# A message-passing layer on one core: bucket regions of a scratch table laid into one another

## The chip, the core and the metric

The kernel runs on one core of a Trainium2 chip. The metric is the device time of one execution in microseconds (us); of several timed runs the median counts. A profile is one further execution under the hardware profiler.

## The reference

The layer works on 12,500 nodes with 64 features and 212,500 edges, sorted by their destination. `src` and `dst` are the two ends of an edge; the sums are made per `src`.

```python
h = jnp.maximum(_layernorm(x, axis=-1), 0.0)
edge_in = jnp.concatenate([h[src], h[dst], edge_weight1], axis=1)
e = jax.nn.silu(edge_in @ eW1 + eb1)
e = jax.nn.silu(e @ eW2 + eb2)
agg = jax.ops.segment_sum(e, src, num_segments=h.shape[0])
node_in = jnp.concatenate([h, agg], axis=1)
x = x + jax.nn.silu(node_in @ nW1 + nb1) @ nW2 + nb2
```

The first matrix product is split: `h @ eW1` of either end is made once per node (the tables `ta` for `src` and `tb` for `dst`, each as three bf16 parts), so that an edge only needs a row of each and its weight times the last row of `eW1`.

## The kernel before, in words

**Buckets.** Nodes are dealt into NB = 100 buckets of L = 125 (node number modulo 100 is the bucket, the quotient is the place in it). Edges come in the order of `dst`, but the sums go by `src`. So edges are first sent to a scratch table in HBM by the bucket of their `src`, and then read back bucket by bucket.

**Chunks.** The edges are cut into blocks of BLK = 1024 and these into 11 chunks (`CHUNKS`, L49): the first has 8 blocks, the others 20 each (the last a little fewer). Each chunk has its own scratch table `q` (L79) of rows of W = 144 floats (576 bytes): 128 floats of the edge's first product so far, and 16 copies of the place of its `src`. A bucket has a region of `cap` x 128 rows in it (cap is 1 in the first chunk, 2 in the others), all of one bucket after one another.

**Zeros.** A bucket doesn't fill its region, so the rows from number `zero` on (48 of 128, then 152 of 256) are written with zeros first. `fill` (L87) does it with DMAs from a tile of zeros, `each` buckets a DMA; a bucket's tail is cut into 64 pieces, one from each of 64 partitions: 234 floats (936 bytes), in the first chunk 180 (720 bytes). Chunk 0's zeros are SP's first DMA (L208); those of chunk c + 1 go out from ACT's queue (L467, 25 buckets a DMA, four DMAs a chunk) in the first blocks of chunk c.

**Prologue** (to L319). SP loads `x`, ACT's queue the edge lists. Layer norm on VectorE and ScalarE, transposes and the table `tb` on TensorE, stores of `tb` and of the transposed `h` (`hd`) by SP. From the edge lists come, per edge, the bucket number of `src` and the place in it, transposed into `bkE` and `locE` (edges on partitions). L313 turns the bucket number b in `bkE` into the last row number before the bucket's region, b * cap * 128 - 1.

**Sending** (`count`, `send`, `send_all`, L389 to L478). For a block of 1024 edges: `load` (L372) brings the block's numbers on all partitions (`bc`), the window of `tb` rows that its `dst` can have (`win`), and the edge weights. VectorE marks the bucket of each edge (L397) and counts the edges of each bucket by a running sum (scan, L400), with the count carried on over the chunk; L407 keeps each edge's own rank, starting with 1. TensorE brings the rank onto the edge's partition by a product with a column of ones (L426) and makes the edge's row from `pick` and `win` (L434). ScalarE copies it to `qs` (L441) and adds the place (L448); VectorE adds rank and region start to the row number `to` (L444); GpSimd scatters 128 rows by an indirect DMA (L453), eight a block, 1661 in all. `qs` has eight buffers of four such tiles.

**Steps.** The scratch table is read in batches of G = 4 buckets. `fetch` (L488) loads a batch's rows from SP's queue (`qt`, L498: on each partition, for each of the four buckets, `n` = cap rows that lie together) and the batch's rows of `ta` (`a3`, L503), NQ = 5 batches ahead. A batch has n steps of 4 x 128 edges; there are 525 steps. A step brings the place onto the columns (`s_lr`, L520), compares (`s_one_t`, L525), adds the transposed row and the `ta` row (`s_pt`, L534 and L541), applies silu (L545), compares the place with the node numbers (`s_one`, L552), makes the second product on top of the bias (L566, L572), applies silu (L576), and sums by place in PSUM (`s_seg`, L586); at the end of a batch `s_add` (L597) adds the sums to `aggT`. Of the last chunk each batch is followed by the node part (`nodes`, L333 to L353).

**Order.** In this main part the order of instructions on TensorE, VectorE, ScalarE and SP is the program's own: `turn` (L604) gives the pieces of a step with how many steps ahead each runs; at six places in it the sending of the next chunk is moved on by so many pieces that the chunk is sent when its first fetch comes (L649 to L667), and `feed` makes the table `ta`, from reloaded parts of `hd` (`hr`, L611), which the first fetches need. While chunk 0 is sent there are no steps yet.

Of the kernel before, what the change touches and what calls it, by code (L numbers as in the profile page):

```python
# [28 lines left out]
F32 = mybir.dt.float32  # L29
F16 = mybir.dt.float16  # L30
# [3 lines left out]
OP = mybir.AluOpType  # L34
# [4 lines left out]
P = 128  # L39
L = 125  # L40
WL = 112
BLK = 1024
# [15 lines left out]
def tile_gnn(ctx: ExitStack, tc: tile.TileContext, x, src, dst, ew, eW1, eb1, eW2, eb2, nW1, nb1, nW2, nb2, out):  # L58
# [14 lines left out]

    chunks = []
    p0 = 0
    for np_, cap, zero in CHUNKS:
# [2 lines left out]
        p0 += np_  # L81


    zeros = const.tile([P, 4 * W], F32, name="zeros")
    nc.gpsimd.memset(zeros, 0.0)

    def fill(c, engine, each):  # L87


        _, _, cap, zero, q = chunks[c]  # L90
        n = (cap * P - zero) * W // 64
        rows = q[: NB * cap * P, :].rearrange("(b s) w -> b s w", s=cap * P)
        for b in range(0, NB, each):
            part = rows[b : min(b + each, NB), zero:, :].rearrange("b s w -> b (s w)")
            part = part.rearrange("b (r n) -> r b n", n=n)
            yield lambda part=part: engine.dma_start(part, zeros[:64, None, :n].to_broadcast(list(part.shape)))

# [48 lines left out]
    nc.vector.tensor_copy(nodes1, nodes_i)  # L146
    ones = const.tile([1, P], F32, name="ones")
    nc.vector.memset(ones, 1.0)
    ones16 = const.tile([P, 1], F16, name="ones16")
    nc.vector.memset(ones16, 1.0)  # L150
    bad = const.tile([P, 2], F32, name="bad")
    nc.vector.memset(bad, 0.0)

# [47 lines left out]
    with tc.tile_pool(name="pro", bufs=1) as pro, tc.tile_pool(name="norm", bufs=2) as np_, tc.tile_pool(  # L201
# [3 lines left out]
        for c0 in range(0, NB, CH):  # L205
            nc.vector.memset(xs[96:, c0 : c0 + CH, :], 0.0)
            rows16(nc.sync.dma_start, xs[:, c0 : c0 + CH, :], x_rows[:, c0 : c0 + CH, :])
        for f in fill(0, nc.sync, NB):  # L208
            f()


# [98 lines left out]
                    nc.scalar.copy(to[:, k0 : k0 + 4, :], tr)  # L310
        for p0, p1, cap, _, _ in chunks:
            v = bkE[:, :, p0:p1]
            nc.vector.tensor_scalar(v, v, float(cap * P), -1.0, op0=OP.mult, op1=OP.add)  # L313


        d3 = pro.tile([P, 3, H], BF16, name="d3")
# [40 lines left out]
    with tc.tile_pool(name="ld", bufs=4) as ld, tc.tile_pool(name="ld2", bufs=NQ) as ld2, tc.tile_pool(  # L357
# [31 lines left out]
        def count(s):  # L389

            if s >= nblocks:
                return
            c = chunk_of[s]
            bc, win, pick = blk[s]
            nc.vector.tensor_scalar(pick[:WL, :], bc[:WL, 0, :], part[:WL, :], None, op0=OP.is_equal)
            oh = wk.tile([NB, BLK], F16, name="oh")
            nc.vector.tensor_scalar(oh, bc[:NB, 1, :], part[:NB, :], None, op0=OP.is_equal)  # L397
            yield
            run = wk.tile([NB, BLK], F16, name="run")
            nc.vector.tensor_tensor_scan(  # L400
                run, oh, nil.to_broadcast([NB, BLK]), carry.get(c, 0.0), op0=OP.add, op1=OP.add
            )
            yield
            n = min(BLK, E - s * BLK)
            end = run[:, n - 1 : n]
            carry[c] = end
            nc.vector.scalar_tensor_tensor(oh, run, 1.0, oh, op0=OP.mult, op1=OP.mult)  # L407
            blk[s].append(oh)
            if s + 1 == nblocks or chunk_of[s + 1] != c:
                u = wk.tile([NB, 1], F32, name="u")  # L410
                for limit, op in ((chunks[c][2] * P, OP.is_gt), (chunks[c][3], OP.is_lt)):
                    nc.vector.tensor_scalar(u, end, float(limit), None, op0=op)
                    nc.vector.tensor_tensor(bad[:NB, 1:2], bad[:NB, 1:2], u, op=OP.add)
            yield

        def send(s):

            p, g = s // 2, s % 2
            c = chunk_of[s]
            _, _, cap, _, q = chunks[c]  # L420
            _, win, pick, run = blk.pop(s)
            n = min(BLK, E - s * BLK)
            nt = -(-n // P)
            rank = misc[:, (s % 2) * TB : (s % 2 + 1) * TB]
            for t in range(nt):
                nc.tensor.matmul(rank[:, t : t + 1], run[:, t * P : (t + 1) * P], ones16[:NB, :], start=True, stop=True)  # L426
            yield
            for t0 in range(0, nt, G):
                qs = qsp.tile([P, G, W], F32, name="qs")
                qp = mm.tile([P, G, H], F32, name="qp", tag="mm")  # L430
                m = min(G, nt - t0)
                for t in range(m):
                    for i in range(3):
                        nc.tensor.matmul(  # L434
                            qp[:, t, :],
                            pick[: WL + 3, (t0 + t) * P : (t0 + t + 1) * P],
                            win[: WL + 3, i, :],
                            start=i == 0,
                            stop=i == 2,
                        )  # L440
                nc.scalar.copy(qs[:, :m, :H], qp[:, :m, :])  # L441
                if t0 == 0:
                    to = top.tile([P, TB], I32, name="to")
                    nc.vector.scalar_tensor_tensor(  # L444
                        to[:, :nt], rank[:, :nt], float(cap * P + 1), bkE[:, g * TB : g * TB + nt, p], op0=OP.min, op1=OP.add
                    )
                at = g * TB + t0
                nc.scalar.copy(  # L448
                    qs[:, :m, H:], locE[:, at : at + m, p][:, :, None].to_broadcast([P, m, W - H])
                )  # L450
                for t in range(t0, t0 + m):
                    k = min(P, n - t * P)
                    i = nc.gpsimd.indirect_dma_start(  # L453
                        out=q[:],
                        out_offset=bass.IndirectOffsetOnAxis(ap=to[:k, t : t + 1], axis=0),
                        in_=qs[:k, t - t0, :],
                        in_offset=None,
                    )

                    tc.declare_no_dep(i.ins, group=f"rows{c}", reason="each edge has a row of its own")  # L460
                    tc.add_to_no_dep_group(f"rows{c}", i.ins)
                yield

        def send_all(c):

            mine = [s for s in range(nblocks) if chunk_of[s] == c]
            zeros_left = list(fill(c + 1, nc.scalar, 25)) if c + 1 < len(chunks) else []  # L467
            each = -(-len(zeros_left) // len(mine))
            for s in mine:
                load(s + 2, 1)  # L470
# [17 lines left out]
        def fetch(i):  # L488
            if i >= len(batches):
                return  # L490
            c, B, n = batches[i]
            assert pending[c] == 0
            while B not in done_a:
                next(feed)
            q = chunks[c][-1]
            at = B * G * n * P
            qt = ld2.tile([P, G * most, W], F32, name="qt")
            nc.sync.dma_start(  # L498
                qt[:, : G * n, :].rearrange("p (b j) w -> p b (j w)", b=G),
                q[at : at + G * n * P, :].rearrange("(b p j) w -> p b (j w)", b=G, p=P),  # L500
            )
# [12 lines left out]
        def s_lr(k):  # L514
            (qt, _, _), tiles = of(k)
# [31 lines left out]

        def s_one(k):
            (qt, _, _), tiles = of(k)
            j = tiles[0][0]  # L550
            one = wk.tile([P, G, L], F32, name="one")
            nc.vector.tensor_tensor(  # L552
                one,
                nodes1[:, None, :].to_broadcast([P, G, L]),
                qt[:, j : j + G, H : H + 1].to_broadcast([P, G, L]),
                op=OP.is_equal,
            )
            st[k]["one"] = one
            c, B, n, g = steps[k]
            if g == n - 1:  # L560
                fetch(c * (NB // G) + B + NQ)

# [259 lines left out]
```

## Time and profile before

| | us |
|---|---|
| median of 3 timed runs | 2777.59 (2777.4 to 2782.52) |
| profiled execution, its own time | 3318.54 |
| its span, first to last instruction | 3316.8 |
| first scatter (L453) starts | 172.5 |
| first step's silu (L545) starts | 303.0 |
| last scatter starts | 3019.2 |

The profiled execution takes longer than the timed ones. On the page, busy times are per engine with their share of the span; PE is TensorE's products, PEld its weight loads, SP only issues DMAs. q1 is SP's DMA queue, q10 ACT's, q0 GpSimd's, q8 brings instructions; the share of a queue is that of all 16 DMA engines over the span. In a table of windows, each engine has its busy time and the number of its instructions; PEclk is the granted clock, then come the DMA engines' mean busy share and GB/s. In a line of a timeline: start, duration, engine and line, and in brackets how long the engine was idle before, and what ended that. A line of the waits gives the total, the number and the longest.

### The profile page before, as it was taken

The page shows a single profiled execution, that of the slowest core. Times are in us where ns is not written, and L with a number is a line of the kernel's source. Part 1 is how long each engine was busy: PE and PEld are TensorE (multiplying, and loading weights), DVE is VectorE, ACT ScalarE, POOL GpSimd, SP SyncE. Part 2 cuts the span into 40 slices and gives each one's busy share as a digit, 9 for nine tenths or more (in the row PEclk, how much of TensorE's full clock was granted, in tenths as well). Part 3 has the DMA queues.
Part 4 walks back from the last instruction along what each step waited for, and adds up shares of the span by engine and source line. Part 5 has one row for each costly group of instructions (what it writes and reads, how often), then busy time and mean ns, then how long its engine had stood idle before and what let it go on. Part 6 is the DMA issues. An engine that isn't in the chain of part 4 may idle for free. (4 is left out here: it accounts for less than half of the span.)

```text
span 3316.8 us, 60674 instructions
## 1 busy us (share of the span) xinstructions
PE 2676.8 (81%) x23583; PEld 2376.4 (72%) x23583; DVE 1891.0 (57%) x2663; ACT 1252.8 (38%) x2663; POOL 1800.1 (54%) x1691
## 2 busy tenths in 40 slices
PE   2575877887888788788888888888887878889998
PEld 1354666777777777777777777777777777778886
DVE  6643565665666566556565655666565656655332
ACT  3422333333343344333333333343333433434443
POOL 1064766666666666566666666656666666662000
PEclk9998777898898988888888888889888888989999
DMA  6567657656755855755675585576557454554441
GB/s 178 183 197 210 199 173 234 194 171 196 227 180 171 247 168 179 233 183 167 191 226 170 176 243 169 166 222 202 179 182 235 160 185 163 185 174 158 133 134 49
DMA packets 388689, 612.83 MB, mean 185 GB/s; under 512 B 47232, under 2 KB 294401, under 8 KB 387877
## 3 DMA queue, kind: packets, MB, share of 16 engines
q1 hardware_dynamic: 269560, 423.47, 40.2%
q0 software_dynamic: 53760, 122.94, 10.7%
q10 hardware_dynamic: 65074, 62.46, 7.6%
q8 instruction: 188, 3.08, 0.4%
q14 instruction: 107, 0.88, 0.1%
HBM read 393.49 MB, written 215.18 MB: 184 GB/s over the span
## 5 line engine op out<-in xcount | busy, mean ns | idle before, releaser
L453 POOL DMA_INDIRECT q<-qs,to x1661 | 1787.4, 1076 | 1203.9 <-ACT qs L448 527.8
L525 DVE TENSOR_SCALAR oneT<-lr,part 125x512 bf16<-125x512 f32 x525 | 392.5, 748 | 666.6 <-remote 251.3
L545 ACT ACTIVATE e<-pt 128x512 f32<-128x512 f32 x525 | 314.7, 599 | 1185.2 <-PE pt L541 349.1
L586 PE MATMUL seg<-one,e 128*128 128x125 f32 x4200 | 658.7, 300 | 75.7 <-issue 63.5
L572 PE MATMUL p<-w,e 128*128 128x128 f32 x4200 | 658.2, 299 | 63.9 <-issue 61.1
L572 PEld LDWEIGHTS p<-w,e 128*128 128x128 f32 x4200 | 582.8, 211 | 105.8 <-issue 97.7
L586 PEld LDWEIGHTS seg<-one,e 128*128 128x128 f32 x4200 | 583.3, 211 | 92.3 <-issue 84.6
L541 PE MATMUL pt<-oneT,a 125*128 125x256 bf16 (+1 forms) x3300 | 498.3, 287 | 67.8 <-issue 65.1
L434 PE MATMUL qp<-win,pick 115*128 115x128 bf16 x4983 | 433.9, 238 | 136.2 <-issue 112.1
L434 PEld LDWEIGHTS <-pick 115*128 115x128 bf16 x4983 | 363.8, 108 | 177.6 <-issue 170.9
L400 DVE TENSOR_TENSOR_SCAN run<-oh,run,misc 100x1024 f16<-100x1024 f16 x197 | 460.9, 2340 | 30.3 <-remote 15.2
L541 PEld LDWEIGHTS <-a 125*128 125x128 bf16 x3300 | 332.2, 105 | 140.8 <-issue 97.5
L534 PE MATMUL pt<-ident,qt 128*128 128x128 f32 x2100 | 365.3, 296 | 76.0 <-DVE oneT L525 38.0
L441 ACT COPY qs<-qp 128x512 f32<-128x512 f32 x416 | 244.0, 586 | 456.8 <-remote 180.0
L597 DVE TENSOR_TENSOR aggT<-aggT,seg 128x500 f32<-128x500 f32 x250 | 168.4, 673 | 394.8 <-PE seg L586 127.0
L576 ACT ACTIVATE e<-p 128x512 f32<-128x512 f32 x525 | 315.4, 601 | 166.8 <-PE pt L534 53.8
L552 DVE TENSOR_TENSOR one<-nodes,qt 128x500 f32<-128x500 f32 x525 | 351.9, 670 | 0.5 <-PE seg L586 0.5
L566 ACT COPY p<-b2f 128x512 f32<-128x512 f32 x525 | 312.9, 596 | 0.0
L534 PEld LDWEIGHTS pt<-ident,qt 128*128 128x128 f32 x2100 | 246.0, 153 | 93.0 <-issue 49.9
L520 PE MATMUL lr<-identb,qt 128*125 128x128 bf16 x2100 | 234.2, 233 | 42.7 <-issue 36.2
L407 DVE SCALAR_TENSOR_TENSOR oh<-run,oh 100x1024 f16<-100x1024 f16 x208 | 253.6, 1219 | 0.0
L520 PEld LDWEIGHTS <-qt 128*125 128x125 bf16 x2100 | 206.0, 149 | 55.7 <-issue 51.0
(117 smaller groups left out, 1266.4 us busy)
## 6 DMA issues: line engine op xcount, KB each, us to landing
qt<-q SPq DMA_DIRECT2D x250, 576.0 KB
a<-ta SPq DMA_DIRECT2D x275, 384.0 KB
bc<-rows SPq DMA_DIRECT2D x208, 448.0 KB
q<-zeros ACTq DMA_DIRECT2D x40, 1462.5 KB
q<-qs,to POOLq DMA_INDIRECT x1661
win<-tb SPq DMA_DIRECT2D x208, 84.0 KB
tb<-parts SPq DMA_DIRECT2D x25, 384.0 KB
ta<-parts SPq DMA_DIRECT2D x25, 384.0 KB
```

Of the source, the lines that this page charges most:

```text
L400: nc.vector.tensor_tensor_scan(run, oh, nil.to_broadcast([NB, BLK]), carry.get(c, 0.0), op0=OP.add, op1=OP.add)
L434: nc.tensor.matmul(qp[:, t, :], pick[: WL + 3, (t0 + t) * P : (t0 + t + 1) * P], win[: WL + 3, i, :], start=i == 0, stop=i == 2,)
L453: i = nc.gpsimd.indirect_dma_start(out=q[:], out_offset=bass.IndirectOffsetOnAxis(ap=to[:k, t : t + 1], axis=0), in_=qs[:k, t - t0, :], in ...
L520: nc.tensor.matmul(lr[:L, t, :], loc[:, at : at + 1].to_broadcast([P, L]), identb, start=True, stop=True)
L525: nc.vector.tensor_scalar(oneT, st[k].pop("lr")[:L], part1[:L, :], None, op0=OP.is_equal)
L534: nc.tensor.matmul(pt[:, t, :], qt[:, j, :H], ident, is_transpose=True, start=t == 0, stop=False, skip_group_check=True)
L541: nc.tensor.matmul(pt[:, cols, :], a3[:L, b, i, :], oneT[:, cols, :], start=False, stop=i == 2, skip_group_check=True)
L545: nc.scalar.activation(e1, pt, AF.Silu)
L552: nc.vector.tensor_tensor(one, nodes1[:, None, :].to_broadcast([P, G, L]), qt[:, j : j + G, H : H + 1].to_broadcast([P, G, L]), op=OP.is_e ...
L572: nc.tensor.matmul(p2[:, t, :], e1[:, t, :], w2, start=False, stop=t == G - 1, skip_group_check=True)
L576: nc.scalar.activation(e2, p2, AF.Silu)
L586: nc.tensor.matmul(item[2][:, b, :], e2[:, t, :], one[:, t, :], start=j % n == 0, stop=j % n == n - 1)
```

## The change

The regions of the four buckets of a batch are laid into one another: row r of bucket b, which had row number b * cap * 128 + r, now has (b // 4) * 4 * cap * 128 + 4 * r + b % 4. So the four buckets' rows that one partition of `qt` takes lie together in HBM, and so do the zeros of four buckets.

- `fetch`: one run of 4 x n rows per partition, 4608 bytes (2304 in the first chunk) in place of four of 1152 (576). Inside `qt` the rows are now ordered by rank and then bucket, so `of` gives other tile numbers, `s_one` reads the places with one more dimension, and `s_seg` starts and stops its sums at other tile numbers.
- `fill`: pieces of 3744 bytes (2880 in the first chunk), in DMAs of 7 groups of four buckets (7, 7, 7, 4) in place of 25 buckets; as many DMAs and bytes as before. The tile of zeros has 936 floats a partition in place of 576.
- The row number needs b // 4: three further VectorE instructions per chunk in the prologue. The rank is multiplied by 4 (`fours` in place of `ones16`), and starts with 0.

```diff
-    zeros = const.tile([P, 4 * W], F32, name="zeros")
+    most_zeros = max((cap * P - zero) * G * W // 64 for _, cap, zero in CHUNKS)
+    zeros = const.tile([P, most_zeros], F32, name="zeros")
...
-        n = (cap * P - zero) * W // 64
-        rows = q[: NB * cap * P, :].rearrange("(b s) w -> b s w", s=cap * P)
-        for b in range(0, NB, each):
-            part = rows[b : min(b + each, NB), zero:, :].rearrange("b s w -> b (s w)")
+        n = (cap * P - zero) * G * W // 64
+        rows = q[: NB * cap * P, :].rearrange("(b s) w -> b s w", s=cap * P * G)
+        for b in range(0, NB // G, each):
+            part = rows[b : min(b + each, NB // G), zero * G :, :].rearrange("b s w -> b (s w)")
...
-    ones16 = const.tile([P, 1], F16, name="ones16")
-    nc.vector.memset(ones16, 1.0)
+    fours = const.tile([P, 1], F16, name="fours")
+    nc.vector.memset(fours, float(G))
...
-        for f in fill(0, nc.sync, NB):
+        for f in fill(0, nc.sync, NB // G):
...
-            nc.vector.tensor_scalar(v, v, float(cap * P), -1.0, op0=OP.mult, op1=OP.add)
+            q4 = np_.tile([P, 2 * TB, p1 - p0], F32, name="q4")
+            nc.vector.tensor_scalar(q4, v, 0.5 - G / 2, 1.0 / G, op0=OP.add, op1=OP.mult)
+            nc.vector.tensor_scalar(q4, q4, float(3 * 2**22), None, op0=OP.add)
+            nc.vector.tensor_scalar(q4, q4, -float(3 * 2**22), None, op0=OP.add)
+            nc.vector.scalar_tensor_tensor(v, q4, float(cap * P * G - G), v, op0=OP.mult, op1=OP.add)
...
-                run, oh, nil.to_broadcast([NB, BLK]), carry.get(c, 0.0), op0=OP.add, op1=OP.add
+                run, oh, nil.to_broadcast([NB, BLK]), carry.get(c, -1.0), op0=OP.add, op1=OP.add
...
-                        to[:, :nt], rank[:, :nt], float(cap * P + 1), bkE[:, g * TB : g * TB + nt, p], op0=OP.min, op1=OP.add
+                        to[:, :nt], rank[:, :nt], float(G * cap * P), bkE[:, g * TB : g * TB + nt, p], op0=OP.min, op1=OP.add
...
-            zeros_left = list(fill(c + 1, nc.scalar, 25)) if c + 1 < len(chunks) else []
+            zeros_left = list(fill(c + 1, nc.scalar, 7)) if c + 1 < len(chunks) else []
...
-                qt[:, : G * n, :].rearrange("p (b j) w -> p b (j w)", b=G),
-                q[at : at + G * n * P, :].rearrange("(b p j) w -> p b (j w)", b=G, p=P),
+                qt[:, : G * n, :].rearrange("p j w -> p (j w)"),
+                q[at : at + G * n * P, :].rearrange("(p j) w -> p (j w)", p=P),
...
-            return batch[c, B], [(g * G + t, (g * G + t) // n) for t in range(G)]
+            return batch[c, B], [((g * G + t) % n * G + (g * G + t) // n, (g * G + t) // n) for t in range(G)]
...
-            j = tiles[0][0]
+            c, B, n, g = steps[k]
+            wide = [P, G // n, n, L]
+            loc = qt[:, : G * n, H : H + 1].rearrange("p (j b) w -> p b j w", b=G)
             one = wk.tile([P, G, L], F32, name="one")
             nc.vector.tensor_tensor(
-                one,
-                nodes1[:, None, :].to_broadcast([P, G, L]),
-                qt[:, j : j + G, H : H + 1].to_broadcast([P, G, L]),
+                one.rearrange("p (b j) l -> p b j l", j=n),
+                nodes1[:, None, None, :].to_broadcast(wide),
+                loc[:, tiles[0][1] : tiles[0][1] + G // n].to_broadcast(wide),
...
-                nc.tensor.matmul(item[2][:, b, :], e2[:, t, :], one[:, t, :], start=j % n == 0, stop=j % n == n - 1)
+                nc.tensor.matmul(item[2][:, b, :], e2[:, t, :], one[:, t, :], start=j < G, stop=j >= G * (n - 1))
```

More of the change, by code (lines that the diff above doesn't have):

```diff
@@ L410, in count @@
                 u = wk.tile([NB, 1], F32, name="u")
-                for limit, op in ((chunks[c][2] * P, OP.is_gt), (chunks[c][3], OP.is_lt)):
+                for limit, op in ((chunks[c][2] * P - 1, OP.is_gt), (chunks[c][3] - 1, OP.is_lt)):
                     nc.vector.tensor_scalar(u, end, float(limit), None, op0=op)
@@ L425, in send @@
             for t in range(nt):
-                nc.tensor.matmul(rank[:, t : t + 1], run[:, t * P : (t + 1) * P], ones16[:NB, :], start=True, stop=True)
+                nc.tensor.matmul(rank[:, t : t + 1], run[:, t * P : (t + 1) * P], fours[:NB, :], start=True, stop=True)
             yield
@@ L558, in s_one @@
             st[k]["one"] = one
-            c, B, n, g = steps[k]
             if g == n - 1:
```

## Prediction

> **What bounds the kernel now.** I read the page first, then a table of windows by stage, the waits, and timelines of the start.
>
> ```profile
> PE 2676.8 (81%) x23583; PEld 2376.4 (72%) x23583; DVE 1891.0 (57%) x2663; ACT 1252.8 (38%) x2663; POOL 1800.1 (54%) x1691
> ...
> DMA packets 388689, 612.83 MB, mean 185 GB/s; under 512 B 47232, under 2 KB 294401, under 8 KB 387877
> ...
> q1 hardware_dynamic: 269560, 423.47, 40.2%
> q0 software_dynamic: 53760, 122.94, 10.7%
> q10 hardware_dynamic: 65074, 62.46, 7.6%
> ...
> L453 POOL DMA_INDIRECT q<-qs,to x1661 | 1787.4, 1076 | 1203.9 <-ACT qs L448 527.8
> ```
>
> No engine is full over the whole span; TensorE is nearest. The queues take 40.2 + 10.7 + 7.6 = 58.5% of the 16 engines, so transfers don't bound the whole, but they may bound a stage.
>
> ```profile
> core 0: us, PE busy (x) PEld busy (x) DVE busy (x) ACT busy (x) POOL busy (x), PEclk, DMA share, GB/s
> 0.00:33.00 33.00, 0.00 (x0) 0.00 (x0) 6.75 (x13) 0.35 (x1) 12.65 (x30) 1.00 0.95 240
> 268.00:303.00 35.00, 9.64 (x58) 7.58 (x59) 12.05 (x17) 4.62 (x12) 8.74 (x8) 1.00 0.94 279
> 1400.00:1800.00 400.00, 328.70 (x3067) 304.39 (x3066) 239.59 (x329) 154.00 (x329) 243.63 (x228) 0.88 0.61 190
> 3050.00:3250.00 200.00, 200.00 (x1510) 164.01 (x1509) 71.33 (x116) 81.39 (x155) 0.00 (x0) 1.00 0.42 131
> ```
>
> Four stages with four limits. In the first 33 us and at 268 to 303 us the DMA engines are full (0.95, 0.94) and TensorE does 0 and 9.6 us of work. In the long middle TensorE is busy 328.7 of 400 us at DMA share 0.61. In the tail it is busy all the time. One stall shows how a full DMA system reaches TensorE:
>
> ```profile
> 273.35 1.83 SPq L498 DMA_DIRECT2D qt<-q  x1
> ...
> 290.02 0.34 SPq L611 DMA_DIRECT2D hr<-hd  x1
> ...
> 296.82 1.22 PE L182 MATMUL ab<-w,hr 64*128 64x128 f32 x4 [21.44 <-DMA hr<-hd]
> ```
>
> SP works in order: five qt and a3 loads hold up the small hr load, and TensorE idles 21.4 us for it.
>
> ```profile
> POOL q L453 <- ACT qs L448: 527.8, 142, 143.7
> POOL q L453 <- issue: 521.3, 1426, 5.9
> ```
>
> In the middle GpSimd takes 1076 ns a scatter and 0.3 us between two when it has a backlog (1426 gaps). The other gaps are waits for ACT, which follows TensorE. The middle of this profile is thus paced by TensorE, with GpSimd close behind. Matmul starts over 0.35 us apart make 102 of the 400 us there, often in clusters where a few matmuls come every 0.7 us and the page says "issue".
>
> The profiled execution took 3318.54 us (span 3316.8), the median of the timed runs is 2777.59, 541 us less. What stretches it isn't shown. If the clusters go, a step of the middle costs TensorE (400 - 102)/72 = 4.1 us (72 steps in the window), while GpSimd needs 160 scatters in 50 steps x 1.376 = 4.4 us. All scatters at that pace, with first scatter at 172 us and the 297 us after the last: 172 + 1661 x 1.376 + 297 = 2755, near 2777. I take the timed middle to be paced by scatters: likely, not shown.
>
> [...] Packet records by size have medians of 29 ns (576 B), 51 (1152), 121 (3072) and 159 (4096), a line of 8.8 ns + 36.7 ns per 1000 B. [...] Here the 239 scatters beside L407 took 1439 ns, the others 1015: what lengthens scatters is mostly VectorE, which the change leaves alone. [...]
>
> **The change, part by part.**
>
> Prices. Each row of a load has one packet in place of four. By the line, 4608 B cost 178 ns where four of 1152 cost 4 x 51 = 204. The recorded mean of 1152 is 65.3 (a few wait long), so a row costs 261 now. After: 178 if the long waits go, 178 + 4 x 14.3 = 235 if they stay. A row saves 26 to 83 ns. Zeros: 936 B have a mean of 60.5 and a floor of 44 (tenth percentile); 3744 B give 146 to 146 + 4 x 16.5 = 212 against 242, so 30 to 96 ns saved.
>
> Zeros at the start (L96, SP's first issue): 6400 packets of mean 48.2 ns / 16 = 19.3 us of the 31.3 us that the engines worked before 33 us. Then 1600 of 2880 B: line 115 ns, with the waits 167: 11.5 to 16.7 us. Saves 2.6 to 7.8; I take 5, all on the path, since edge lists and x land behind it.
>
> Zeros for later chunks: 40 DMAs, each 1600 x 60.5 / 16 = 6.05 us, then 3.65 to 5.3. Three of the first four lie at 172 to 230 us (share 0.82 to 0.85), one at 152 to 161: 4 x 0.75 to 2.4 = 3 to 9.6; I take 6. Two lie in the full window at 268, with five qt loads of 512 packets (34.7 ns each, 1.1 us a load; 128 packets of 2304 B: 93 to 116 ns, saves 0.2 to 0.4): 2.4 to 6.8, taken as 4. Two more at 303 to 340 run beside TensorE: 2.
>
> The 32 fills of chunks 3 to 10 take about 9 us each on the clock. In 20 us stretches of the middle where q10 has over 0.3, matmul starts are 7.22 per us against 7.69 without it: 6% of 290 us = 18 us. A fill a third shorter gives 6 to 7.
>
> qt loads in the middle: 250 loads, 128,000 packets, 522 us of engine time, then 356 to 470. They are fetched five batches ahead, and by the view of the tile qt they end 6.4 us of waits in all: worth nothing on the path, cover being this lead. With the lead gone it would be 52 to 166 us of engine time.
>
> Added: 4 VectorE instructions per chunk in place of 1 (44 for 11). From these rows, 0.16 us each, 5.4 us more:
>
> ```profile
> 104.67 0.95 DVE L313 TENSOR_SCALAR bkE<-bkE 128x64 f32<-128x64 f32 x6
> ...
> 115.79 0.76 DVE L187 TENSOR_TENSOR prest<-ab,parts 128x256 f32<-128x256 f32 x2 [6.79 <-ACT parts L183]
> ```
>
> The 6.8 us idle right behind hides them: ACT waits there for tb stores. Cost 0; without cover 5.4, and the first scatter is late by it. No wait is added, and PE, ACT, POOL and SP keep their orders. L552 reads 500 elements as before with another dimension: 0, at most 525 x 0.1 = 52 us of VectorE time, which at 57% is off the path. Memset of 936 in place of 576: 0.36 us. Scatters are as many and as large: 0.
>
> Sum: 5 + 6 + 4 + 2 + 7 = 24 us. All but 7 are stages before 340 us that don't depend on the middle's pace, so I take it off the median as it is: 2777.6 - 24 = **2753 us**. Bounds: 12 (low prices, little on the path) to 40 (high prices, SP freed sooner at 268): 2738 to 2766.
>
> **Rivals.**
> (1) *Hidden.* The start's savings end in another wait: edge lists behind GpSimd's chain of small loads, the hr load behind ta and bc. For it: SP waits on buffers everywhere. Against: share 0.95 and 0.94. About 2777.
> (2) *Transfers matter in the middle too.* Saved engine time: qt 52 to 166, fills 30 to 96, the rest 7 to 17; middle near 180 us. If four tenths reach the clock: 2777 - 73 = 2704. For it: at the timed pace share rises to 0.585 x 3317 / 2777 = 0.70. Against: stretches of share 0.55 to 0.7 run as fast as those under 0.55 (7.73, 7.76 starts per us).
> (3) *Slower: larger packets hold up instructions.* [...] qt has 74 of 243 us of engine time in the middle, on the clock 0.19 of it; with exposed fetches and fills' share (0.08 x 0.4): 188 x (0.10 + 0.03) = 24 us, so 2802. It decides once fetch comes too late, that is if the clusters of slow issue are late fetches. For it: VectorE and GpSimd go on during them. Against: q8's packets don't fall at their starts, and the tail fetches at full pace without one.
>
> **How the numbers follow.** Forecast 0.50, hidden 0.20, transfers 0.16, slower 0.14. No change is within 0.2% (5.6 us), about what a measurement of this kernel can tell. Faster: 0.48 + 0.16 + 0.03 of hidden's edge = 0.67; same 0.19; slower 0.14. Range: down to 2700 (half of the transfer case), up to 2785 (hidden, with uncovered 5.4 us of VectorE work).
>
> **What would show it.** q1 at about 159,000 packets (147,200 fewer, 36,800 in their place) and q10 near 17,000, their shares down; 0 to 33 us with VectorE's first reduction (35.87) at about 31; the stall for hr at 268 to 303 shorter; first scatter (172) earlier by 5 to 11; in 1400 to 1800 us unchanged step time; scatters still 1076 ns; tail 10.4 us per batch. Wrong if the first scatter doesn't move, or the middle's step time moves by over 2%.

## The result, and the profile after

| | kernel before | changed kernel |
|---|---|---|
| median, us (7 runs each) | 2781.91 | 2793.36 |
| range | 2777.4 to 2786.84 | 2786.67 to 2796.86 |
| ratio, 95% interval | | 1.0041 [1.0027, 1.0055] |
| profiled execution, own time | 3318.54 | 2793.36 |
| first VectorE reduction of the edge lists starts | 35.9 | 40.3 |
| first scatter starts | 172.5 | 176.3 |

The change costs 11 us (8 to 15). The forecast was 24 us less, 2753.

The kernel before takes some 2780 us on some chips and 3320 to 3400 on others, so a time below is only set against kernels that ran beside it on the same chip. The profile of before is from a chip of the slow sort, and the profile after from one of the other, so I compare the two only before 180 us. Even there they differ in the clock granted to TensorE: from 105 to 172 us it is 1.00 in the one and 0.50 in the other. This clock differs from profile to profile of one kernel, and the first scatter doesn't follow it: the changed kernel has its first scatter at 174.3 us in e6 (clock 1.00) and at 174.0 in e16 (clock 0.50). The ratios below are the recorded ones; the quotient of the medians beside them can differ from them by up to 0.2%.

The page of the changed kernel, in the lines that answer to those shown of before:

```profile
PE 2335.9 (84%) x23583; PEld 2178.7 (78%) x23583; DVE 1889.9 (68%) x2696; ACT 1263.6 (45%) x2663; POOL 1800.5 (64%) x1691
...
DMA packets 230289, 612.83 MB, mean 220 GB/s; under 512 B 47232, under 2 KB 83201, under 8 KB 229477
...
q1 hardware_dynamic: 159160, 423.47, 46.9%
q0 software_dynamic: 53760, 122.94, 13.0%
q10 hardware_dynamic: 17074, 62.46, 8.7%
...
L460 POOL DMA_INDIRECT q<-qs,to x1661 | 1787.7, 1076 | 681.5 <-issue 433.0
```

The packets are what was foreseen: q1 has 159,160 in place of 269,560, q10 17,074 in place of 65,074. The bytes are the same. What the packets cost isn't: 46.9% of 2791.6 us is 1309 us of time on q1's engines, where 40.2% of 3316.8 was 1333; q10 has 243 for 252. With 158,000 packets fewer the transfers take 2% less time, not the tenth that I had priced. Packet records by size say the same:

| packets | floor | mean, ns | engine time in all, us |
|---|---|---|---|
| qt 1152 B, before | 51 | 65.3 | 522 |
| qt 4608 B, after | 178 | 239.3 | 479 |
| zeros 936 B, before | 44 | 60.5 | 242 |
| zeros 3744 B, after | 146 | 232.5 | 232 |
| zeros 720 B, before | 35 | 48.2 | 19.3 |
| zeros 2880 B, after | 114 | 181.3 | 18.1 |

The floors (tenth percentiles) lie where the line of sizes put them. But the time above the floor, which I took to be a few long waits for each packet, grew with the packet, and more than fourfold: 16.5 ns for 936 B, 86.5 for 3744. Of the slow packets the same can be said: the ninetieth percentiles are 79 and 318 ns, four times the time for four times the bytes.

The waits of GpSimd, of the changed kernel (total, number, longest):

```profile
POOL q L460 <- issue: 433.0, 1415, 1.3
POOL q L460 <- ACT qs L455: 163.8, 22, 140.0
```

Here the scatters do pace the middle: 1415 gaps of 0.3 us with nothing awaited, and 22 waits for ACT, the longest that ahead of the first scatter. In the trace of before there were 142 such waits. From scatter 224 on, 160 scatters start 1.35 to 1.41 us apart on average, as 1.376 was foreseen. A scatter still takes 1076 ns.

The windows of the changed kernel:

```profile
core 0: us, PE busy (x) PEld busy (x) DVE busy (x) ACT busy (x) POOL busy (x), PEclk, DMA share, GB/s
0.00:33.00 33.00, 0.00 (x0) 0.00 (x0) 6.75 (x13) 0.00 (x0) 12.33 (x29) 1.00 0.93 248
268.00:303.00 35.00, 16.96 (x146) 14.19 (x146) 14.86 (x21) 9.20 (x20) 13.65 (x15) 0.60 0.84 275
1400.00:1800.00 400.00, 357.29 (x3957) 347.74 (x3958) 303.52 (x415) 201.16 (x425) 311.44 (x289) 0.95 0.77 248
```

The start is as full as before (0.93 for 0.95). In it lies the first sign of where time was lost. GpSimd loads small weights and waits for several of them to land; behind them on its queue stands the padding for the edge lists (pad_i, pad_f), which ACT's queue sends ahead of ACT's first cast. First the two waits that grew, in the timeline of GpSimd of the kernel before:

```profile
17.22 0.49 POOL L131 DMA_DIRECT2D nb2r<-in_L_gnn_nb_dram  x1 [1.90 <-DMA w2n<-in_L_gnn_nW_dram]
...
28.30 0.50 POOL L218 MEMSET pad_f<- 1x492 f32 x1 [7.52 <-DMA srcR<-pad_i]
```

and of the changed one:

```profile
21.44 0.48 POOL L133 DMA_DIRECT2D nb2r<-in_L_gnn_nb_dram  x1 [4.79 <-DMA w2n<-in_L_gnn_nW_dram]
...
35.77 0.50 POOL L220 MEMSET pad_f<- 1x492 f32 x1 [10.96 <-DMA srcR<-pad_i]
```

The wait for the weight w2n ends 4.2 us later, and the 492 padding numbers take 3.4 us longer to land. The packets beside these small loads are now 2880 B of zeros at a mean of 181 ns, where they were 720 B at 48. That the small loads are late because of them is a theory so far; how an engine shares its time among the queues isn't in the traces. That the lists of dst and src land early helps nothing: their last packets on ACT's queue end at 12.6 us (11.8 before), but ACT's cast of dstR stands behind the issue of pad_f in its order. The issue starts at 36.29 us (31.85 before), the cast at 38.38 (33.94).

### The profile page after: what moved, and what is told of

Read it like the earlier page. It is cut to its first block, busy times and chain, and to the rows that moved or that the text cites. A ratio compares the mean times of both kernels' runs of the same rounds, so it can differ in the third digit from the quotient of the medians.

```text
span 2791.6 us, 60708 instructions
## 1 busy us (share of the span) xinstructions
PE 2335.9 (84%) x23583; PEld 2178.7 (78%) x23583; DVE 1889.9 (68%) x2696; ACT 1263.6 (45%) x2663; POOL 1800.5 (64%) x1691
## 3 DMA queue, kind: packets, MB, share of 16 engines
q1 hardware_dynamic: 159160, 423.47, 46.9%
q10 hardware_dynamic: 17074, 62.46, 8.7%
## 4 chain that ended last, share of the span: by engine, by line
PE 52%; DMA 15%; POOL 13%; issue 10%; DVE 7%; ACT 2%; SPq 1%; DVEq 0%; ACTq 0%; POOLq 0%
POOL q L460 13%; PE seg L595 12%; PE p L581 11%; DMA q<-qs,to 8%; PE pt L549 8%; PE qp L441 6%; PE pt L542 6%; PE lr L528 3%; DVE run L407 3%; DMA hr<-hd 2%; DMA tb<-parts 1%; PE z L349 1%; PE ab L184 1%; DMA q<-zeros 1%; DMA qt<-q 1%
## 5 line engine op out<-in xcount | busy, mean ns | idle before, releaser
L460 POOL DMA_INDIRECT q<-qs,to x1661 | 1787.7, 1076 | 681.5 <-issue 433.0
L581 PE MATMUL p<-w,e 128*128 128x128 f32 x4200 | 580.6, 282 | 114.3 <-ACT p L575 114.3
L581 PEld LDWEIGHTS p<-w,e 128*128 128x128 f32 x4200 | 526.1, 197 | 129.3 <-ACT p L575 116.3
L595 PE MATMUL seg<-one,e 128*128 128x125 f32 x4200 | 584.8, 283 | 30.1 <-DVE aggT L606 24.9
L595 PEld LDWEIGHTS seg<-one,e 128*128 128x128 f32 x4200 | 526.0, 197 | 33.8 <-ACT e L585 18.5
L549 PE MATMUL pt<-oneT,a 125*128 125x256 bf16 (+1 forms) x3300 | 443.3, 273 | 0.0
L441 PE MATMUL qp<-win,pick 115*128 115x128 bf16 x4983 | 371.3, 228 | 47.7 <-DVE oneT L533 43.4
L441 PEld LDWEIGHTS <-pick 115*128 115x128 bf16 x4983 | 332.1, 103 | 56.2 <-issue 51.5
L542 PE MATMUL pt<-ident,qt 128*128 128x128 f32 x2100 | 332.9, 282 | 25.3 <-DVE oneT L533 23.5
L528 PE MATMUL lr<-identb,qt 128*125 128x128 bf16 x2100 | 212.1, 225 | 65.4 <-DMA qt<-q 65.4
L528 PEld LDWEIGHTS <-qt 128*125 128x125 bf16 x2100 | 188.8, 141 | 66.9 <-DMA qt<-q 66.2
```

What stands on the lines that cost most here:

```text
L441: nc.tensor.matmul(qp[:, t, :], pick[: WL + 3, (t0 + t) * P : (t0 + t + 1) * P], win[: WL + 3, i, :], start=i == 0, stop=i == 2,)
L460: i = nc.gpsimd.indirect_dma_start(out=q[:], out_offset=bass.IndirectOffsetOnAxis(ap=to[:k, t : t + 1], axis=0), in_=qs[:k, t - t0, :], in ...
L528: nc.tensor.matmul(lr[:L, t, :], loc[:, at : at + 1].to_broadcast([P, L]), identb, start=True, stop=True)
L542: nc.tensor.matmul(pt[:, t, :], qt[:, j, :H], ident, is_transpose=True, start=t == 0, stop=False, skip_group_check=True)
L549: nc.tensor.matmul(pt[:, cols, :], a3[:L, b, i, :], oneT[:, cols, :], start=False, stop=i == 2, skip_group_check=True)
L581: nc.tensor.matmul(p2[:, t, :], e1[:, t, :], w2, start=False, stop=t == G - 1, skip_group_check=True)
```

## The experiments

The theories to tell apart. **Start**: chunk 0's large zero packets make the small loads late, and that goes through to the end. **Zeros**: large zero packets in the middle hold up something. **Rows**: the layout or the 4608-byte reads cost. All of it can be small, so a time beside it has to be known within some 5 us.

### Parts of the change alone

e1 is the kernel before with all zeros in large packets: a bucket's tail is cut into 16 pieces in place of 64, which then come from partitions 0 to 15.

```diff
-        n = (cap * P - zero) * W // 64
+        n = (cap * P - zero) * W // 16
...
-            yield lambda part=part: engine.dma_start(part, zeros[:64, None, :n].to_broadcast(list(part.shape)))
+            yield lambda part=part: engine.dma_start(part, zeros[:16, None, :n].to_broadcast(list(part.shape)))
```

> The kernel before, with only the zeros' packets made large (16 pieces of 3744 bytes a bucket in place of 64 of 936; 2880 in place of 720 in the first chunk); rows keep their regions and are loaded in packets of 1152. Theory Z (the large packets of zeros hold up small transfers in the first 340 us, before the scatters set the pace): slower by 8 to 12 us, ratio 1.003 to 1.0045. Theory R (the interleaved rows or their packets of 4608 bytes cost it): ratio 1.000.

e3 does it in chunk 0 alone.

> The kernel before, with only chunk 0's zeros in packets of 2880 bytes. Theory Z: first scatter about 4 us later, 2 to 5 us slower, ratio 1.001 to 1.002. Theory R: ratio 1.000, and the late first scatter of the changed kernel comes from something else.

e2 is the changed kernel with the zeros of chunks 1 to 10 in 936-byte packets.

```diff
+        if c:
+            n = n // G
+            for k in range(G):
+                part = rows[:, zero * G :, :].rearrange("b s w -> b (s w)")
+                part = part.rearrange("b (k r n) -> r k b n", n=n, k=G)[:, k]
+                yield lambda part=part: engine.dma_start(part, zeros[:64, None, :n].to_broadcast(list(part.shape)))
+            return
```

> The changed kernel, with the zeros of chunks 1 to 10 in packets of 936 bytes again (as many DMAs as before, each over all 25 groups); rows interleaved, chunk 0's zeros in packets of 2880. Theory Z: chunk 0's zeros keep about 4 us (the first reduction of the changed kernel came at 40.3 us against 35.9), ratio 1.0015. Theory R: ratio 1.004 as the changed kernel.

e4 is the changed kernel with chunk 0's zeros behind the inputs: a small VectorE instruction that writes zeros into the tile of zeros makes their DMA wait for the edge lists.

```diff
-        for f in fill(0, nc.sync, NB // G):
-            f()
...
+        nc.vector.tensor_scalar(zeros[:NP, 0:1], lo[:, 0:1], 0.0, None, op0=OP.mult)
+        for z in fill(0, nc.sync, NB // G):
+            z()
```

> The changed kernel, with chunk 0's zeros issued behind the inputs (they wait for the first reduction of the edge lists, some 40 us in), so that edge lists, x and weights have the first 33 us for themselves: 19 us of engine time leave this stage. If the start up to the first scatter is on the path of the whole: first scatter 10 to 18 us earlier than in the changed kernel (176.3), total 5 to 18 us faster than it, ratio to before 0.998 to 1.002. If the start is absorbed later, no change from 1.004.

| beside before at 3397.7 us | median | ratio, interval | first reduction | first scatter |
|---|---|---|---|---|
| e1 zeros alone | 3584.56 | 1.0546 [1.0509, 1.0583] | 59.0 | 213.1 |
| e3 zeros of chunk 0 alone | 3439.11 | 1.0131 [1.0094, 1.0168] | 59.9 | 208.6 |
| e2 rows, and zeros of chunk 0 | 3400.93 | 1.0017 [1.0002, 1.0033] | 38.1 | 173.9 |
| e4 zeros late | 3403.01 | 1.0010 [0.9992, 1.0028] | 36.8 | 176.5 |

e1 and e3 don't tell the theories apart, but show two other things. e3's windows:

```profile
core 0: us, PE busy (x) PEld busy (x) DVE busy (x) ACT busy (x) POOL busy (x), PEclk, DMA share, GB/s
...
30.00:40.00 10.00, 0.00 (x0) 0.00 (x0) 0.00 (x0) 0.00 (x0) 0.49 (x1) 1.00 0.96 104
```

The engines are busy at 0.96 and move 104 GB/s. The 2880-byte zero packets have a mean of 388 ns here, against 181 in the changed kernel; e1's 3744-byte ones 529 against 232. The size is the same, only the source differs: 16 neighbouring partitions in place of 64. The packets take 2.1 to 2.3 times as long. From 16 partitions eight apart, in e12 below, the 2880-byte packets take 177 ns, as from 64. So a fill's time goes with bytes and source partitions; what makes neighbouring partitions slow isn't shown.

What zeros from 64 partitions take when they have the engines nearly for themselves is seen in e4 and e8, which send chunk 0's zeros from 65 to 89 us. A window of e8:

```profile
core 0: us, PE busy (x) PEld busy (x) DVE busy (x) ACT busy (x) POOL busy (x), PEclk, DMA share, GB/s
...
70.00:80.00 10.00, 2.89 (x10) 1.59 (x10) 7.59 (x11) 5.76 (x8) 0.00 (x0) 1.00 0.98 204
```

Full engines move 204 GB/s there, and the 2880-byte packets take 219 to 227 ns (tenth and ninetieth percentile), nearly twice the floor of 114 that they have in the mixed traffic of the start. So the floor isn't what a fill costs. By their means, 16 engines do 16 x 936 / 60.5 = 248 GB/s of zeros in small packets and 16 x 3744 / 232.5 = 258 in large ones: the size of the packet hardly counts. This is why the fills saved next to nothing. That the source sets the limit is shown for 16 neighbouring partitions alone (388 and 177 ns). What limits zeros from 64 isn't shown: no run sends them from all 128.

Second, e3's first scatter is 36 us late, and its time 41 us over: a delay of that size in the start goes to the end in full.

What spoils e1 and e3 further is the order of the prologue's instructions, in these two and in e4, e8, e11 and e12: the framework sets that order, and with one DMA changed it came out otherwise. In e3 the edge numbers are worked on before the layer norm. The start of such a kernel doesn't tell what the packets alone do. The prologue of the changed kernel keeps the order of before, and so do e2, e10 and e13 to e18.

### The same kernels again

> The kernel before, unchanged, for a profile on one chip with the changed kernel: its profile so far (3316.8 us) and the timed runs beside the changed kernel (2781.9) are of different chips, and in the second profile the clusters of slow TensorE issue are gone. Theory S (the 11 us arise in the start, up to about scatter 384, and the scatters pace the rest at 1.376 us in both kernels): first scatter here about 4 us earlier than in the changed kernel, scatter 384 about 10 us earlier, then the same pitch. Theory M (the middle pays): scatter 384 at the same time, pitch shorter by 0.6%. Ratio 1.000.

> The changed kernel, unchanged, on the same chip as the run before it. Ratio 1.003 to 1.005 on a chip without the clusters of slow issue; with them, no theory gives a number, and the ratio itself is what is wanted.

> The changed kernel with the zeros of chunks 1 to 10 in packets of 936 bytes again, once more, beside the changed kernel itself. If large packets of zeros in the start cost 7 of the 11 us: 7 us faster than the changed kernel, ratio to before 1.0015. If not: as the changed kernel.

> The changed kernel with chunk 0's zeros behind the inputs, once more, beside the changed kernel itself. If the small loads [...] cost the first 4 us: first reduction at or before 36 us, 4 to 10 us faster than the changed kernel. If the start's 4 us have another cause: no change.

| beside before at 3318.79 us | median | ratio, interval | first reduction | first scatter |
|---|---|---|---|---|
| e5 before again | 3323.26 | 1.0010 [0.9991, 1.0029] | 36.3 | 172.8 |
| e6 after again | 3325.80 | 1.0020 [1.0002, 1.0039] | 38.4 | 174.3 |
| e7 as e2 | 3321.85 | 1.0012 [0.9992, 1.0032] | 39.2 | 176.1 |
| e8 as e4 | 3326.53 | 1.0005 [0.9986, 1.0024] | 36.4 | 176.4 |

Nothing can be told apart by time: the kernel before differs from itself by 0.1%, and e6's 0.2% is clear of no change by a hair, but not of e5. The start can. Late zeros bring the first reduction back to 36.4, but the first scatter stays at 176.4: they now lie beside the stores of tb.

Profiles from these chips have TensorE's slow clusters, of both kernels. In the first profile of before, between 600 and 3000 us, a matmul starts 0.35 to 1.6 us behind the one before it some 740 times, 565 us in all; in the profile after, between 520 and 2500 us, 17 times, 11 us. They go with the chips, not with the change. Their cause stays open.

### Light kernels

To let the scatters pace the middle on any chip, four kernels leave out part of TensorE's work.

```diff
-                for i in range(3):
+                for i in (2,):
...
-            for t in range(G):
-                nc.tensor.matmul(
-                    p2[:, t, :], e1[:, t, :], w2, start=False, stop=t == G - 1, skip_group_check=True
-                )
```

> The kernel before with part of TensorE's work left out: the second product's four matmuls of a step (the bias alone stays), and only one of the three bf16 parts of the ta row is added. Transfers, scatters, VectorE's and ScalarE's work stay. A step then needs some 3.0 us of TensorE, under the 4.4 us of its 3.2 scatters, so the scatters pace the middle whatever TensorE's issue does, and single runs should lie closer together. It is the base of the next three, whose times are to be compared with its, not with the full kernel's: some 2600 to 2760 us.

> The changed kernel with the same TensorE work left out. If the loss lies in the start or in the scatters, 8 to 14 us slower than the light kernel before; if it lay in TensorE's part of the steps, within 3 us of it.

> The light kernel before with large zero packets alone (3744 and 2880 bytes, 16 pieces a bucket, from 16 partitions spread over the 128), rows in 1152-byte packets as before. If large zero packets in the start and in the middle cause the loss, 8 to 11 us slower than the light kernel before; if the rows laid into one another do, within 3 us of it.

> The light kernel before with chunk 0's zeros alone in 2880-byte packets, from 16 partitions spread over the 128. If these packets delay the small loads of the start, first reduction and first scatter 2 to 4 us later, and the end with them: 2 to 5 us slower than the light kernel before. If the start doesn't matter, within 2 us.

These ran on a chip where the full kernel before takes 2782.27.

| | median, us | against e9 | first reduction | first scatter | first to last scatter |
|---|---|---|---|---|---|
| e9 light before | 2745.78 | | 36.0 | 171.4 | 2351.8 |
| e10 light after | 2759.82 | +14.0 | 39.7 | 176.2 | 2356.7 |
| e11 light, all zeros large | 2770.66 | +24.9 | 39.0 | 187.7 | 2363.4 |
| e12 light, zeros of chunk 0 large | 2765.40 | +19.6 | 39.9 | 188.6 | 2351.9 |

The differences of the medians are uncertain by about 7 us; the other columns are from one profile each. e10 repeats the loss, with TensorE's part left out, so TensorE's steps aren't its place. Its first scatter is 4.8 us late, and between first and last scatter it loses 4.9 more, 4.2 of them before scatter 224. From there to the last scatter e9 and e10 take 2013.1 and 2013.8 us. (e9's profiled run is 5.7 us over its median, and takes 226 us behind the last scatter where the other three take 219 to 221. So the profiled runs of e9 and e10 themselves differ by 4 us only.) e12's first scatter is 17.2 us late (more than the packets explain, by the other order), and its scatters then stay 13 to 21 us behind e9's to the end: a delay of that size isn't made up.

e11 and e12 have the same order and differ only in the zeros of chunks 1 to 10 (3744 bytes from 16 partitions eight apart, or 936 from 64): 11.5 us between first and last scatter, 5.3 (within 4.7) in the medians. GpSimd's waits for earlier scatters to land, between 520 and 2500 us, of e9 and e12 (small zeros in the middle):

```profile
POOL q L453 <- DMA q<-qs,to: 24.4, 80, 0.3
```

```profile
POOL q L454 <- DMA q<-qs,to: 24.5, 80, 0.4
```

and of e10 and e11 (large):

```profile
POOL q L460 <- DMA q<-qs,to: 31.0, 86, 2.2
```

```profile
POOL q L454 <- DMA q<-qs,to: 33.4, 90, 1.2
```

With small zeros no such wait is over 0.4 us. With large ones some take 1 to 2. Of all gaps between scatters 224 and 1600, whatever ended them, those over 0.5 us number 1 in e9, 1 in e12, 12 in e10 and 12 in e11 (0.9, 0.6, 11.2 and 14.4 us), and all 26 end 7 to 20 us behind the issue of a fill. In the 20 us behind a fill, 14.38 and 14.36 scatters start with small zeros, 14.21 and 14.17 with large: 0.18 x 1.4 us is a quarter of a microsecond a fill, 8 for the 32 fills of that stretch. e10 gets most of it back, at about 14.25 scatters in 20 us elsewhere against 14.15 to 14.2 in the other three. It is the one with 4608-byte reads. e11's lag doesn't grow evenly, though: at scatter 832 it has passed 7 us of such gaps and is no further behind e12 than at the first scatter, and all the lag comes after. So the gaps go with the large zeros, but that they make the 11.5 us isn't shown.

One more place is the stage from 268 us. TensorE's waits for the reloaded hr, of e9 and of e10:

```profile
PE ab L182 <- DMA hr<-hd: 49.6, 8, 12.1
```

```profile
PE ab L184 <- DMA hr<-hd: 54.0, 8, 13.3
```

They were to become shorter, and didn't. Nor do the 4.4 us more say much: e17 below, which reads chunk 0 in small packets again, waits 53.7 us here, and e18, which reads it in large ones, 49.8. From the first scatter to scatter 224, e9, e11 and e12 take 338.7, 337.6 and 338.1 us, e10 342.9. e11 has the large fills there too, so this would be the rows, if single profiles could be trusted to 4 us. They can't: in the full kernels on such chips the sign is the other, 350.8 us in e17 and 346.1 and 347.1 in the changed kernel and e18.

### With the prologue's order kept

e13 undoes the change in chunk 0 alone, zeros, rows and reads.

```diff
+        if c == 0:
+            n = (cap * P - zero) * W // 64
+            rows = q[: NB * cap * P, :].rearrange("(b s) w -> b s w", s=cap * P)
...
+            if p0 == 0:
+                nc.vector.tensor_scalar(v, v, float(cap * P), None, op0=OP.mult)
+                continue
...
+            if c == 0:
+                nc.sync.dma_start(
+                    qt[:, : G * n, :].rearrange("p (b j) w -> p b (j w)", b=G),
+                    q[at : at + G * n * P, :].rearrange("(b p j) w -> p b (j w)", b=G, p=P),
+                )
```

> The changed kernel with chunk 0 as in the kernel before: its zeros in 720-byte packets, its rows not laid into one another. Theory Z0 (chunk 0's large zero packets delay the small loads of the start, and that is all): first reduction at 36 us, first scatter at 171 to 172 us, the time within 3 us of the kernel before, 8 to 11 us under the changed kernel. Theory M (something of chunks 1 to 10 costs most of it): first scatter as early, but the time 5 to 9 us over the kernel before.

e14 adds e2's edit to it.

> As e13, and the zeros of chunks 1 to 10 in 936-byte packets too, so only the rows' layout in chunks 1 to 10 and the 4608-byte reads of qt are left of the change. If e13 is slower than the kernel before by 5 us or more: here within 3 us of the kernel before when the zeros of these chunks do it, as slow as e13 when the rows do it. If e13 is like the kernel before, this one is too.

e15 takes away pad_f's wait.

```diff
-        pad_f = pro.tile([1, PAD], F32, name="pad_f", tag="pad_i")
-        nc.gpsimd.memset(pad_f, 0.0)
+        pad_f = zeros[:1, :PAD]
```

> The changed kernel, with the 492 zeros behind the last edge weights taken from the tile of zeros, in place of a tile pad_f whose memset waits until pad_i has landed in srcR. ScalarE's issue of ewR from pad_f then doesn't wait (it stood 5.2 us in the changed kernel's profile), so the first cast and the first reduction come some 5 us earlier (35 to 36 us in place of 40), the first scatter at 171 to 173. If the start passes through to the end, 3 to 6 us faster than the changed kernel; if the loss is only in the middle, within 2 us of it.

> The changed kernel once more, as the base of these three: first reduction at 38 to 40 us, first scatter at 174 to 176, and 0.2 to 0.5% slower than the kernel before.

| beside before at 3324.06 us | median | ratio, interval | first reduction | first scatter |
|---|---|---|---|---|
| e13 chunk 0 as before | 3324.53 | 1.0001 [0.9981, 1.0021] | 36.6 | 173.7 |
| e14 rows of chunks 1 to 10 alone | 3331.97 | 1.0003 [0.9977, 1.0029] | 36.2 | 173.1 |
| e15 no wait for pad_f | 3326.00 | 0.9994 [0.9964, 1.0023] | 35.1 | 170.6 |
| e16 after again | 3328.29 | 1.0010 [0.9980, 1.0040] | 38.0 | 174.0 |

Again the times tell nothing, and the start does what the theory says of it. So e13 and e15 ran once more, and met a chip of the other sort.

> The kernel of e13 again, the changed kernel with chunk 0 as before. Where the kernel before takes some 2780 us: within 3 us of it if chunk 0's large packets are the whole loss, with the first scatter at 171 to 172 us and scatter 224 as early as before; 4 to 8 us over it if the rows laid into one another cost something between scatters 64 and 224. Where it takes some 3320 us, nothing within 5 us can be told.

> The kernel of e15 again, the changed kernel without the wait of pad_f's memset. First reduction at 35 us, first scatter at 170 to 172. Where the kernel before takes some 2780 us: 4 to 8 us over it, if the start's delay (4 to 5 us) is gone and the rest of the loss stays; as slow as the changed kernel (some 11 us over) if the start isn't on the path.

| beside before at 2782.88 us | median | ratio, interval | first reduction | first scatter |
|---|---|---|---|---|
| e17 chunk 0 as before | 2795.39 | 1.0047 [1.0032, 1.0061] | 36.5 | 172.5 |
| e18 no wait for pad_f | 2790.26 | 1.0024 [1.0011, 1.0037] | 36.1 | 172.4 |

In e17's timeline of GpSimd the two waits are shorter again, the first by a third of what it had grown, the second by nine tenths:

```profile
19.37 0.96 POOL L140 DMA_DIRECT2D nb2r<-in_L_gnn_nb_dram  x2 [3.76 <-DMA w2n<-in_L_gnn_nW_dram]
...
29.39 0.50 POOL L229 MEMSET pad_f<- 1x492 f32 x1 [7.81 <-DMA srcR<-pad_i]
```

And yet e17 is 12.5 us over the kernel before (8.9 to 17.0). **The theory Start falls as the cause of the whole.** The delay is there and e17 is without it, but the time doesn't follow. Its lead of 3.8 us over the changed kernel's profile (of another chip, of the same sort) at the first scatter is 1.6 at scatter 64, gone at 224, and both start their last scatter at 2505 us. e18, as early at the first scatter, has 7.4 us over (3.1 to 10.3), about what was expected of it; in its profile the lead at the first scatter, 3.9 us, is 2.9 at scatter 224 and 0.3 at the last. The two differ by 5.1 us (within 3.6); e18 has chunk 0's rows in large packets and e17 hasn't. That those give back some of the stage from 268 us would fit these profiles, but not e9 and e10, and no run shows it alone.

So most of the loss comes with chunks 1 to 10. The light pair e11 and e12 hints at one way: large zeros hold up scatters. In the full kernels that sign is weak: the changed kernel has 3 gaps over 0.5 us with 2.2 us in all, e17 has 5 with 3.9, e18 1 with 2.1, and no profile of the full kernel before is from such a chip. Where in the full kernel the 11 us arise, and whether zeros or rows cost more, **stays open**. e14 was to tell and ran only where it couldn't. No version came out that beats the kernel before.

## Why the prediction was wrong

**Prices: failed, and all else with them.** "30 to 96 ns saved" for 3744 B of zeros: measured 4 x 60.5 - 232.5 = 9.5; in e9 and e10, on one chip, the zeros of chunks 1 to 10 take 247.6 and 242.5 us of engine time. "A row saves 26 to 83 ns": 22. I had taken the floor as what a packet costs, and the time above it as waits that fewer packets might lose, or at worst keep. Even that worst case, 4 x 16.5 = 66 ns above the floor, was too good for the zeros: the large packet spends 86.5 there. What each packet costs by itself shows only at the floor (4 x 44 against 146). Zeros that have the engines for themselves don't run at the floor but at 204 GB/s (e8), and at half of that from 16 neighbouring partitions (104, e3): there the bytes count.

**Zeros at the start, "5, all on the path": wrong sign.** In six profiles with 720-byte packets and the same order (before, e5, e9, e13, e14, e17) the first reduction starts at 35.9 to 36.6, mean 36.2; in six with 2880-byte packets (after, e2, e6, e7, e10, e16) at 38.0 to 40.3, mean 38.9. First scatter: 172.7 and 175.1. So 2.5 us were lost at the first scatter, where 5 to 11 were to be won. The wait named in the first rival, "edge lists behind GpSimd's chain of small loads", is the one; I had it hide the gain, but it turned the sign.

**Fills at 150 to 340 us, "6", "4" and "2": not there.** From the first scatter to scatter 224 the light kernels take 338.7 us before and 342.9 after. The 12 weren't won; whether the 4 are a loss, single profiles can't tell. The hr stall didn't shrink.

**"A fill a third shorter gives 6 to 7": not there.** Fills do end sooner, but by less: the zeros of chunks 3 to 10 are under way for 330 us in e9 and e12, and for 288 and 295 in e10 and e11, a tenth to an eighth less. Nothing was won by it: from scatter 224 to the last, e10 takes as long as e9, and e11 takes 12 us longer than e12.

**What held.** Packets of q1 and q10; the middle paced by scatters, as was "likely, not shown", and scatters of 1076 ns; qt "worth nothing on the path" as far as waits show: TensorE's waits for qt are 75.9 us in e9 and 75.3 in e10. The 33 added VectorE instructions cost nothing. Of the 6.79 us that hid them 2.21 are left:

```profile
119.56 0.76 DVE L189 TENSOR_TENSOR prest<-ab,parts 128x256 f32<-128x256 f32 x2 [2.21 <-ACT parts L185]
```

and the first scatter of the changed kernel is later by 3.8 us, less than the 4.4 of the first reduction.

**The rivals.** The slower one was right in that something ends later beside large packets, and had the wrong victim: instruction fetch at the clusters, which are there without large packets too, while it is small loads that end later (w2n by 4.2 us), and perhaps scatters. Its 24 us, twice the loss, were my estimate, and the fetches don't show it: the 188 packets of q8, of 16,384 B each, take 1068 ns on average before and 1112 after. Transfers that matter in the middle needed the engine time that wasn't saved.

## What to carry to other kernels

Before you count on larger packets, divide bytes by mean packet time. Here the small packets did 248 GB/s, where their floor would have given 16 x 936 / 44 = 340. That distance was the sign that the floor is the wrong price: the large packets came to 258, where theirs would have given 16 x 3744 / 146 = 410. Then look at what else the engines serve in that stage: beside the large packets a chain of small loads that wait for one another ended later, and the first reduction with it, by 2.7 us. A lead or a delay of the start is worth only what the pacing stage keeps of it: in single profiles, 17 us stayed (e12), 4 didn't (e17, e18).

## What the runs showed that I had not expected

- Zeros from 16 neighbouring partitions took twice as long per packet as from 64 (388 ns in e3 and 181 in the changed kernel, for 2880 B); from 16 partitions eight apart they took 177 (e12).
- Zeros from 64 partitions that have the DMA engines nearly for themselves move 204 GB/s, half of what the floor of their packets in mixed traffic would give (16 x 2880 / 114 = 404).
- The clock granted to TensorE between 105 and 172 us is 1.00 in one profile and 0.50 in another of the same kernel (e6 and e16), and the first scatter is as early with either.
- One kernel takes 2780 us on some chips (12 and 15) and 3320 to 3400 on others (2, and 13 with 3319 at one time and 3398 at another), by clusters of matmuls that come slowly. On the former, single runs scatter by 4 us (one standard deviation), on the latter by 10.
- With another shape of one DMA in the prologue the framework ordered the instructions around it anew: e12's first reduction is 3.9 us late, its first scatter 17.2.
